# A four-layer graph network on one core: another order for the first quads (projections into the first softmax's wait, W2's sums earlier, the second softmax's sorting in one group)

## The chip, the cores and the metric

The kernel runs on one core of a Trainium2 chip. The metric is the device time of one execution, in microseconds (us). The kernel before takes 3154.85 us (median of three runs, 3150.97 to 3155.34). Every run that was taken in several rounds is on record as fast, that is, not slowed down as a whole. For the times of the five single looks (e2, e3, e4, e7, e9) no state is on record, so I read steps from their traces and conclude nothing from their times.

## The reference, cut to what matters

Four graph layers run on 128 batch elements of 128 nodes with 256 features. Each adds its result to its input and normalises it.

```python
# layer 0: attention over 512 edges (src -> dst), 4 heads
Xq, Xv = x @ W_lin.T, x @ W_val.T
e = sum(leaky_relu(Xq[:, src] + Xq[:, dst]) * a) + log(adj[src, dst] + eps)
attn = softmax of e over the edges with the same src
x = layernorm(x + segment_sum(attn * Xv[:, dst], src) @ W_out.T)
# layer 1: three graph convolutions with adj*adj, W1 (256->512), W2 (512->1024), W3 (1024->256)
# layer 2: three products with W[0..2], mixed by diag / upper / lower part of adj
# layer 3: normalised adj, W1 (256->512), batch norm, relu, W2, batch norm: needs all elements first
```

## The kernel before

Batch elements go in quads of four, 32 quads in all. A loop pass overlaps five quads at different layers; the order of instructions is fixed by hand on every engine. What this study touches is the head: `start()` (quads 0 to 3 up to the softmaxes) and `iteration_0()` (the first, partly filled pass). These are the helpers that the argument needs:

```python
def values_in(k, xg, copy): ...    # TensorE transposes of quad k's input, copies on ScalarE
def values(k, i, copy, ...): ...   # TensorE: projections Xq, Xv of element i; after i == 3 spill Xq to memory
def gather_one(k, t, c, ...): ...  # GpSimd: indirect transfer, chunk c of 128 edges (t=0: src rows, t=1: add dst rows)
def score(k, c, ...): ...          # VectorE, 3.7 us: leaky relu, times a, sum over a head
def sorted_scores(k, perm, ...): ... # TensorE: puts the edges in the order of src
def softmax_parts(k): ...          # generator: scan, scan, subtract (VectorE), Exp (ScalarE), scan, scan
def attention(k): ...              # TensorE transposes, VectorE divides: the attention weights
def scatter(k): ...                # GpSimd: 4 indirect writes, each waiting for the one before; then SyncE loads
                                   # the dense 1 MB attention matrix back
def by_row(k, j, ...): ...         # reorders a quarter of that matrix (ScalarE, or VectorE)
def aggregate(k): ...              # TensorE: attention matrix times values
def second(k, between): ...        # the 1024x512 product W2, 14 parts; between[i]: other work after part i
```

The parts of `start()` and `iteration_0()` in question, with cuts:

```python
            ...
            nc.scalar.activation(weight, weight, AF.Ln)
            score(0, 0)
            ...
            values_in(1, quads[1].xr, nc.scalar.copy)
            ...
            sorted_scores(0, perm, range(NE - 1))
            score(0, NE - 1, ends[:, 3, :])
            sorted_scores(0, perm, (NE - 1,))
            ...  # first softmax
            values_in(2, quads[2].xr, nc.scalar.copy)
            ...
            attention(0)
            values(2, 0, nc.scalar.copy, qt=...)
            scatter(0)
            ...
            score(1, 1, ends[:, 3, :])
            values(3, 1, nc.scalar.copy)
            second_sums()                       # four sums of halves of W2, VectorE
            for j in range(QB):
                by_row(0, j, None if j == 2 else nc.vector.tensor_copy)
            aggregate(0)
            stage_a(0)
            values(3, 2, nc.scalar.copy)
            values(3, 3, nc.scalar.copy)        # its spill goes out on SyncE's queue
            mix1(0, 0)
            ...
            late_loads()                        # layer 2's weights, bias, W3, hidden weights, quad 4, norm vectors
            ...
        def iteration_0():
            late_sums(0)
            between = {i: [] for i in range(14)}
            between[0] = [lambda: attention(1), lambda: scatter(1)]
            for c, i in ((0, 1), (1, 3), (2, 6)):
                between[i].append(lambda c=c: score(2, c))
            between[1].append(lambda: gather_last(2))
            for j, i in enumerate((10, 11, 12, 13)):
                between[i].append(lambda j=j: by_row(1, j))
            second(0, between)
            score(2, NE - 1)
            ...
```

## Time and profile before

| | kernel before |
|---|---|
| median of three runs | 3154.85 us |
| profiled span | 3149.4 us |
| TensorE busy, whole span | 3077.0 us (98%) |
| TensorE idle, 0 to 185 us | 32.9 us |
| TensorE idle, 185 to 3090 us | 27 us |
| first 128x384 product of layer 2 | starts at 175.99 us |

From about 175 us on the program is a steady stream of matmuls. The start of the first 128x384 product of layer 2 is therefore a good mark. Whatever the head gains is the shift of that mark; I call it "the mark" below. The prediction shows and reads the rows of the profile that carry this. One more view matters for what came later. It is SyncE's queue of the kernel before: start, duration, line, transfer.

```profile
61.53 0.34 SPq L427 DMA_DIRECT2D ad<-attd  x1
83.51 0.32 SPq L268 DMA_DIRECT2D qd<-qt  x1
83.88 1.08 SPq L1112 DMA_DIRECT2D l2w<-in_l_w_dram  x2
```

The queue takes its transfers in order. Quad 3's spill (`qd`) waits for projections that are computed near 80 us, so the weight loads behind it start at 83.9 us.

### The profile page before, as it was taken

The page shows a single profiled execution, that of the slowest core. Times are in us where ns is not written, and L with a number is a line of the kernel's source. Part 1 is how long each engine was busy: PE and PEld are TensorE (multiplying, and loading weights), DVE is VectorE, ACT ScalarE, POOL GpSimd, SP SyncE. Part 2 cuts the span into 40 slices and gives each one's busy share as a digit, 9 for nine tenths or more (in the row PEclk, how much of TensorE's full clock was granted, in tenths as well). Part 3 has the DMA queues.
Part 4 walks back from the last instruction along what each step waited for, and adds up shares of the span by engine and source line. Part 5 has one row for each costly group of instructions (what it writes and reads, how often), then busy time and mean ns, then how long its engine had stood idle before and what let it go on. Part 6 is the DMA issues. An engine that isn't in the chain of part 4 may idle for free. (4 is left out here: it accounts for less than half of the span.)

```text
span 3149.4 us, 39744 instructions
## 1 busy us (share of the span) xinstructions
PE 3077.0 (98%) x14752; PEld 2403.3 (76%) x14752; DVE 2306.6 (73%) x4600; ACT 1376.0 (44%) x2548; POOL 651.5 (21%) x535
## 2 busy tenths in 40 slices
PE   7899999999999999999999999999999999989998
PEld 3678888888888888888888888888888887864444
DVE  7777777777777777777777777777777776447888
ACT  3344433444444444334344444444444344326668
POOL 2311222222121111122222211111122220001235
PEclk8999999999999999999999999999999999999999
DMA  5623333333333332333333333332333331005557
GB/s 179 160 68 88 101 108 97 106 108 108 101 86 103 104 91 79 98 108 101 101 108 108 103 94 92 107 91 76 97 108 101 101 108 41 21 31 195 173 195 275
DMA packets 117473, 340.04 MB, mean 108 GB/s; under 512 B 14881, under 2 KB 51617, under 8 KB 108961
## 3 DMA queue, kind: packets, MB, share of 16 engines
q0 software_dynamic: 44544, 147.88, 19.4%
q1 hardware_dynamic: 70976, 188.71, 17.0%
q8 instruction: 117, 1.92, 0.3%
q10 hardware_dynamic: 1760, 0.92, 0.1%
q14 instruction: 76, 0.61, 0.1%
HBM read 252.00 MB, written 85.46 MB: 107 GB/s over the span
## 5 line engine op out<-in xcount | busy, mean ns | idle before, releaser
L575 PE MATMUL ph<-m,w 128*128 128x256 f32 x2048 | 475.0, 380 | 0.0
L655 PE MATMUL p<-w,h 128*128 128x256 f32 x2048 | 463.8, 380 | 0.0
L575 PEld LDWEIGHTS ph<-m,w 128*128 128x128 f32 x2048 | 387.9, 191 | 78.4 <-issue 14.8
L655 PEld LDWEIGHTS p<-w,h 128*128 128x128 f32 x2048 | 389.7, 190 | 67.0 <-issue 8.1
L336 POOL DMA_INDIRECT zs<-qd,src_idx x120 | 117.2, 977 | 1347.8 <-DMA qd<-qt 1216.1
L575 PE MATMUL ph<-m,w_s 128*128 128x256 f32 x1536 | 357.5, 379 | 0.0
L575 PEld LDWEIGHTS ph<-m,w_s 128*128 128x128 f32 x1536 | 291.8, 190 | 52.9 <-issue 14.8
L336 POOL DMA_INDIRECT zs<-qd,dst_idx x120 | 188.1, 1568 | 352.5 <-DMA zs<-qd,src_idx 327.2
L581 ACT COPY u<-ph 128x512 f32<-128x512 f32 x128 | 74.8, 584 | 356.1 <-PE ph L575 356.1
L418 POOL DMA_INDIRECT attd<-at,att_idx x128 | 142.7, 1115 | 347.4 <-DMA attd<-at,att_idx 245.0
L591 ACT ACTIVATE h<-h 128x512 f32<-128x512 f32 x192 | 121.1, 630 | 135.6 <-DVE h L587 135.6
L113 ACT ACTIVATE ln_sd<-ln_mv,eps 128x2 f32<-128x2 f32 x192 | 55.9, 291 | 281.6 <-DVE ln_mv L108 277.8
L370 DVE TENSOR_TENSOR zs<-zs,a_bc 128x1024 f32<-128x1024 f32 x125 | 153.1, 1225 | 4.3
L371 DVE TENSOR_REDUCE scores<-zs 128x16 f32<-128x1024 f32 x125 | 152.5, 1220 | 4.3
L718 ACT COPY x2k<-y 128x384 f32<-128x384 f32 x192 | 92.0, 479 | 138.3 <-PE y L711 113.8
L368 DVE SCALAR_TENSOR_TENSOR zs<-zs 128x1024 f32<-128x1024 f32 x125 | 151.4, 1211 | 0.1
L106 DVE BATCH_NORM_STATS2 ln_st<-xr 128x6 f32<-128x256 f32 x384 | 144.5, 418 | 6.6
L121 DVE TENSOR_SCALAR xr<-xr,ln_mv,ln_rs 128x256 f32<-128x256 f32 x384 | 143.2, 415 | 7.0
L587 DVE TENSOR_TENSOR h<-ph,u 128x512 f32<-128x512 f32 x128 | 87.1, 680 | 73.1 <-PE ph L575 55.0
L437 ACT COPY adc<-ad 128x512 f32<-128x512 f32 x125 | 133.1, 1065 | 4.1 <-DMA ad<-attd 4.1
L679 POOL TENSOR_TENSOR xb<-xr,bias 128x512 f32<-128x512 f32 x64 | 99.3, 1551 | 160.0 <-DVE xr L121 150.7
L532 PE MATMUL pm<-wt_t,h 128*128 128x128 f32 x1024 | 126.7, 277 | 0.0
(342 smaller groups left out, 6071.1 us busy)
## 6 DMA issues: line engine op xcount, KB each, us to landing
ad<-attd SPq DMA_DIRECT2D x32, 1024.0 KB, 4.8
zd<-z SPq DMA_DIRECT2D x31, 1024.0 KB, 7.3
zl<-zd SPq DMA_DIRECT2D x62, 512.0 KB, 3.8
xr<-in_x_dram SPq DMA_DIRECT2D x32, 512.0 KB, 7.5
x3d<-xr SPq DMA_DIRECT2D x32, 512.0 KB, 2.6
x3l<-x3d SPq DMA_DIRECT2D x32, 512.0 KB, 5.1
out_dram<-x3l POOLq DMA_DIRECT2D x31, 512.0 KB
qd<-qt SPq DMA_DIRECT2D x30, 512.0 KB, 2.6
```

The costliest lines, as they stand in the source:

```text
L106: nc.vector.bn_stats(st[:, i, :], r[:, i, :])
L121: nc.vector.tensor_scalar(r[:, i, :], r[:, i, :], mv[:, i, 0:1], rs[:, i:i + 1], op0=ALU.subtract, op1=ALU.mult)
L336: nc.gpsimd.indirect_dma_start(out=s.z[c], out_offset=None, in_=s.qd, in_offset=bass.IndirectOffsetOnAxis(ap=idx[:, c:c + 1], axis=0), com ...
L368: nc.vector.scalar_tensor_tensor(z, z, SLOPE, z, op0=ALU.mult, op1=ALU.max)
L370: nc.vector.tensor_mul(z3, z3, a_bc.unsqueeze(1).to_broadcast([P, QB, D]))
L371: nc.vector.reduce_sum(s.es[:, c, :], z.rearrange("p (r d) -> p r d", d=DH), axis=AX.X)
L418: nc.gpsimd.indirect_dma_start(out=ad, out_offset=bass.IndirectOffsetOnAxis(ap=att_idx[:, c:c + 1], axis=0), in_=s.at[:, c, :], in_offset= ...
L437: (copy or nc.scalar.copy)(s.adc[:, j * H:(j + 1) * H, :], s.ad.rearrange("p (s r) -> p r s", r=R)[:, j * H:(j + 1) * H, :])
L532: nc.tensor.matmul(pm[:, c // 2, c % 2, :], quads[k].h1[i, c], wt_t, start=True, stop=True)
L575: nc.tensor.matmul(bank[g][:, i].rearrange("p b n -> p (b n)"), wa[:, c, f:f + P], s.m2[:, blk_b, c].rearrange("p b n -> p (b n)"), start= ...
L591: nc.scalar.activation(h, h if src_ is None else src_, AF.Relu)
L655: nc.tensor.matmul(p3[:, t * D:(t + 1) * D], s.h2[f // 2][:, f % 2, j + t, :], w3_sb[:, f, :], start=(f == 0), stop=(f == K2 - 1))
```

## The change

The intent is to give TensorE work in its three waits for a softmax and in its wait for the first attention matrix, and to keep its clock up where no work is left. These are the core parts of the diff (small moves and the matching removals are cut):

```diff
+            values_in(1, quads[1].xr, nc.scalar.copy)          # ahead of the logarithm
             nc.scalar.activation(weight, weight, AF.Ln)
...
             score(0, NE - 1, ends[:, 3, :])
+            values_in(2, quads[2].xr, nc.scalar.copy)
             sorted_scores(0, perm, (NE - 1,))
...
+            for i in range(3):
+                values(2, i, nc.scalar.copy, qt=qt2)
             attention(0)
-            values(2, 0, nc.scalar.copy, qt=...)
...
+            for i in range(1, QB):
+                values(3, i, nc.scalar.copy)                   # all of quad 3, ahead of aggregate(0)
...
             second_sums()                                      # both scores of quad 1 now stand ahead of it
+            keep_running(20)                                   # 20 products of ones, result unused
             for j in range(QB):
                 by_row(0, j, None if j == 2 else nc.vector.tensor_copy)
             aggregate(0)
             stage_a(0)
-            values(3, 2, nc.scalar.copy)
-            values(3, 3, nc.scalar.copy)
             mix1(0, 0)
...
-            sorted_scores(1, perm, range(NE - 1))
...
-            sorted_scores(1, perm, (NE - 1,))
+            late_loads()                                       # without W3
...
+            sorted_scores(1, perm)
+            nc.sync.dma_start(w3_sb, w3.rearrange("(c p) f -> p c f", p=P))
...
-            between[0] = [lambda: attention(1), lambda: scatter(1)]
-            for c, i in ((0, 1), (1, 3), (2, 6)):
+            for c, i in ((0, 0), (1, 3), (2, 6)):
                 between[i].append(lambda c=c: score(2, c))
-            between[1].append(lambda: gather_last(2))
+            between[2] += [lambda: attention(1), lambda: scatter(1)]
+            between[3].append(lambda: gather_last(2))
...
-            attention(2)                                       # moved behind w.p3()
-            scatter(2)
```

In the last part the steps of the third softmax are spread between the seven products of `first_seven`. Its Exp stands ahead of the sixth product. One move that is cut above matters later: quad 1's last two gathers (chunks 2 and 3) used to be issued chunk by chunk; now GpSimd issues the first halves of both and then the second halves.

More of the change, by code (lines that the diff above doesn't have):

```diff
@@ L1022, in iteration_0 @@
             mix1(1, 0)
+            next(rest)
             mix1(1, 2)
-            next(rest)
             w = first_seven(1)
             steps = softmax_parts(2)
-            for _ in range(4):
-                next(steps)
+            next(steps)
+            next(rest)
             w.p1()
             next(steps)
+            next(steps)
             run(w.p5, w.p2)
+            next(steps)
+            next(steps)
+            w.p6()
+            next(rest, None)
+            w.p7()
             for _ in steps:
                 pass
-            next(rest)
+            third_mix(0, 2)
+            w.p4()
+            w.p3()
             attention(2)
@@ L1038, in iteration_0 @@
             gather_last(3)
-            w.p6()
-            next(rest, None)
-            w.p7()
-            third_mix(0, 2)
-            w.p4()
-            w.p3()
             quads[0].layer2 = layer2(0, 1)
@@ L1058, in start, with keep_running @@
             nc.scalar.dma_start(a_bc, bass.AP(tensor=a.tensor, offset=a.offset, ap=[[0, P], [1, D]]))
-            warm = ps("warm")[:, :N]
-            for _ in range(10):
-                nc.tensor.matmul(warm, ones, ones, start=True, stop=True)
+            def keep_running(n):
+                warm = ps("warm")[:, :N]
+                for _ in range(n):
+                    nc.tensor.matmul(warm, ones, ones, start=True, stop=True)
+            keep_running(10)
             pos = scratch("pos")
@@ L1114, in late_loads @@
                 nc.sync.dma_start(bias, bass.AP(tensor=l2_bias.tensor, offset=l2_bias.offset, ap=[[0, P], [1, D]]))
-                nc.sync.dma_start(w3_sb, w3.rearrange("(c p) f -> p c f", p=P))
                 nc.sync.dma_start(l3w1, l3_w1_t.rearrange("(c p) f -> p c f", p=P))
@@ L1152, in start @@
             nc.vector.tensor_scalar(es[:, 0, :], es[:, 0, :], ends[:, 3, 0:1], None, op0=ALU.add)
-            values_in(1, quads[1].xr, nc.scalar.copy)
             values(1, 0, nc.scalar.copy)
@@ L1196, in start @@
             sums = wk.tile([P, 6], F32, tag="sums", name="sums", bufs=1)
-            values_in(2, quads[2].xr, nc.scalar.copy)
             pr = ps("adjt_ps")[:, :N]
@@ L1202, in start @@
             nc.vector.tensor_add(an, a_sb, ident)
+            qt2 = l3w1_s.rearrange("p t f -> p (t f)").rearrange("p (b d) -> p b d", d=D)
+            for i in range(3):
+                values(2, i, nc.scalar.copy, qt=qt2)
             attention(0)
-            values(2, 0, nc.scalar.copy, qt=l3w1_s.rearrange("p t f -> p (t f)").rearrange("p (b d) -> p b d", d=D))
             scatter(0)
@@ L1214, in start @@
             nc.vector.reduce_sum(sums[:, 1:2], diag, axis=AX.X)
-            values(2, 1, nc.scalar.copy)
             pr = ps("col_ps")[:, :1]
             nc.tensor.matmul(pr, an, ones[:, 0:1], start=True, stop=True)
+            nc.gpsimd.tensor_copy(small[0][:, 0:1], quads[0].ad[:, 0:1])
+            values(2, 3, nc.scalar.copy, spill_by=nc.gpsimd)
+            for t in range(2):
+                for c in (2, 3):
+                    gather_one(1, t, c, cols_i[:, t, :])
+            values_in(3, quads[3].xg, nc.scalar.copy)
+            score(1, 0, ends[:, 3, :])
             nc.vector.tensor_add(sums[:, 2:3], sums[:, 0:1], pr)
             nc.vector.tensor_sub(sums[:, 3:4], sums[:, 2:3], sums[:, 1:2])
+            values(3, 0, nc.scalar.copy)
             nc.scalar.activation(sums[:, 4:5], sums[:, 3:4], AF.Sqrt)
-            score(1, 0, ends[:, 3, :])
-            values(2, 2, nc.scalar.copy)
-            nc.gpsimd.tensor_copy(small[0][:, 0:1], quads[0].ad[:, 0:1])
-            values(2, 3, nc.scalar.copy, spill_by=nc.gpsimd)
-            for c in (2, 3):
-                for t in range(2):
-                    gather_one(1, t, c, cols_i[:, t, :])
+            score(1, 1, ends[:, 3, :])
             dinv = sums[:, 5:6]
@@ L1231, in start @@
             nc.vector.tensor_scalar(diag, an, dinv, None, op0=ALU.mult)
-            values_in(3, quads[3].xg, nc.scalar.copy)
-            values(3, 0, nc.scalar.copy)
+            for i in range(1, QB):
+                values(3, i, nc.scalar.copy)
             pr = ps("half_ps")[:, :N]
@@ L1236, in start @@
             nc.vector.tensor_scalar(ahat_t, pr, dinv, None, op0=ALU.mult)
-            score(1, 1, ends[:, 3, :])
-            values(3, 1, nc.scalar.copy)
             second_sums()
+            keep_running(20)
             for j in range(QB):
@@ L1243, in start @@
             stage_a(0)
-            values(3, 2, nc.scalar.copy)
-            values(3, 3, nc.scalar.copy)
             mix1(0, 0)
+            first(0, 0)
+            score(1, 2, ends[:, 3, :])
+            first(0, 1)
             mix1(0, 2)
-            score(1, 2, ends[:, 3, :])
-            sorted_scores(1, perm, range(NE - 1))
-            first(0, 0)
+            mixed(0, 0, mix2(0, 0))
+            late_loads()
+            first(0, 2)
             score(1, NE - 1, ends[:, 3, :])
             gather(2)
-            first(0, 1)
-            mixed(0, 0, mix2(0, 0))
-            sorted_scores(1, perm, (NE - 1,))
-            late_loads()
-            first(0, 2)
+            first(0, 3)
             mixed(0, 1, mix2(0, 1))
+            sorted_scores(1, perm)
+            nc.sync.dma_start(w3_sb, w3.rearrange("(c p) f -> p c f", p=P))
+            pm = mix2(0, 2)
             steps = softmax_parts(1)
@@ L1261, in start @@
                 next(steps)
-            first(0, 3)
+            mixed(0, 2, pm)
             next(steps)
-            mixed(0, 2, mix2(0, 2))
             mixed(0, 3, mix2(0, 3))
```

## The prediction

> **What bounds the kernel now.** I read the busy times by stretch first, because the change touches only the head of the program (everything up to the first full loop pass).
>
> ```profile
> 0.00:185.00 185.00, 152.12 (x631) 101.36 (x632) 135.81 (x252) 65.01 (x125) 59.60 (x55) 0.93 0.55 156
> 185.00:3090.00 2905.00, 2878.01 (x13898) 2274.53 (x13897) 2120.92 (x4162) 1258.78 (x2305) 557.55 (x446) 1.00 0.35 102
> 3090.00:3149.40 59.40, 46.92 (x224) 27.42 (x224) 49.89 (x189) 52.24 (x119) 34.39 (x34) 0.94 0.70 253
> ```
>
> After the stretch and its length come the busy times of TensorE, its weight loads, VectorE, ScalarE and GpSimd, then the granted TensorE clock, the DMA share and GB/s. From 185 us to 3090 us TensorE idles 27 us of 2905: that stage is TensorE's, and the change leaves it alone. So the change is worth exactly as much as the start of the full-speed stage moves to the left. In the first 185 us TensorE idles 185 - 152.1 = 32.9 us. The second view is TensorE's waits in these 185 us (total us, times, longest):
>
> ```profile
> PE pat L408 <- DVE pair L400: 14.7, 3, 6.0
> PE py L451 <- DVE adc L437: 7.9, 1, 7.9
> PE pe L360 <- DVE scores L373: 2.7, 2, 1.4
> PE pq L259 <- ACT xt L247: 2.1, 2, 1.8
> PE pm L476 <- DVE xr L121: 1.7, 1, 1.7
> ```
>
> The three waits of the attention transposes for the end of a softmax, and the one wait of the first aggregation for the reordered attention matrix, are 22.6 us of the 32.9. Third, TensorE's timeline shows that a wait also costs afterwards:
>
> ```profile
> 47.75 0.63 PE L408 MATMUL pat<-ident,pair 48*128 48x48 f32 x4 [5.37 <-DVE pair L400]
> 48.31 5.96 PE L259 MATMUL pq<-wqv,xt 128*128 128x512 f32 x8
> ...
> 70.86 3.68 PE L451 MATMUL py<-adc,m 128*64 128x128 f32 x32 [7.90 <-DVE adc L437]
> 74.47 4.85 PE L465 MATMUL po<-wo,yt 128*128 128x256 f32 x16
> 79.16 3.60 PE L259 MATMUL pq<-wqv,xt 128*128 128x512 f32 x8
> ...
> 105.78 0.42 PE L408 MATMUL pat<-ident,pair 48*128 48x48 f32 x4 [3.39 <-DVE pair L400]
> ...
> 161.49 0.63 PE L408 MATMUL pat<-ident,pair 48*128 48x48 f32 x4 [5.97 <-DVE pair L400]
> ...
> 174.59 0.67 PE L697 MATMUL pt<-ident,xr 128*128 128x128 f32 x4 [1.22 <-DVE xr L121]
> ```
>
> Eight projection matmul records take 5.96 us behind the first wait and 3.60 us at 79.16. The fourth view, the clock in short stretches, says why: it is halved there.
>
> ```profile
> 44.00:48.00 4.00, 0.25 (x3) 0.28 (x4) 3.48 (x9) 1.57 (x3) 3.18 (x2) 0.76 0.67 143
> 48.00:52.00 4.00, 4.00 (x9) 1.84 (x9) 2.28 (x9) 0.00 (x0) 1.02 (x1) 0.50 0.95 179
> 72.00:76.00 4.00, 4.00 (x28) 3.40 (x26) 0.00 (x0) 1.17 (x2) 2.59 (x2) 0.50 0.42 55
> ```
>
> From these means the half clock lay over work for about 4.7 us (47.7 to 52.4), 5.9 (70.9 to 76.8), 3.4 (107.5 to 110.9) and 4.0 (161.5 to 165.5): 18 us, half of it lost, 9 us. Idle and cold clock together are 42 us, and that bounds the gain: 42/3155 = 1.3%. A verdict of over 2% is out of reach unless something breaks.
>
> Last, VectorE and ScalarE around the two attention matrices:
>
> ```profile
> 65.46 1.22 DVE L181 TENSOR_TENSOR w_s<-w 128x1024 f32<-128x1024 f32 x1
> ...
> 70.13 1.63 DVE L437 COPY adc<-ad 128x512 f32<-128x512 f32 x3
> ...
> 127.47 1.07 ACT L437 COPY adc<-ad 128x512 f32<-128x512 f32 x1 [1.49 <-DMA ad<-attd]
> ```
>
> ScalarE had its part of the first matrix at 66.29, so the matrix had landed. VectorE reached it only at 70.13, after W2's four sums (4.7 us). The second matrix arrives at 127.4, only just in time.
>
> **What the Trainium skill says.** "TensorE: Matmul & The Clock Gate", Part 1 (the HAM clock gate): after an idle window of about 3.4 us the clock goes to one half, and it needs about 3.4 us of work to come back. The trace agrees: idle from 42.4, half clock from about 46.1, back 4.7 us after work began. The same Part 1 says that ScalarE and VectorE take their instructions strictly in order; the trace agrees (ScalarE's copies of the first transposed inputs stand behind the logarithm at 24.23, and TensorE waits 1.79 us for them). "ScalarE: Activation LUTs", What ACT_TABLE_LOAD costs: about 1283 ns a load; the trace has 1.28 us before each first Exp or Sqrt. It adds a drain of about 1.38 us, of which the trace shows none (load at 156.93, Exp at 158.22). "DMA: Bandwidth & Descriptors", Issuing engines are not separate DMA queues: all share the same engines, so a load let go earlier meets other traffic. DMA shares of 0.95 to 1.05 around 48 to 52 and 100 to 108 show where that can bite.
>
> **The change part by part**, with the durations of the trace, as a schedule in the new program order.
>
> *Copies before the logarithm.* The copies start at 22.9 rather than 24.34, so the 1.79 us wait shrinks to about 0.4. VectorE is solid from 22 to 40 and the softmax still ends at 47.6, so by itself this moves nothing later; it lets quad 1's spill and gathers go about 1.4 us earlier.
>
> *Projections into the first softmax.* Transposes of quad 2 (1.04 us) go into the wait for the last score; three projections (3 x 1.8 = 5.4 us) into 41.5 to 46.9. The 5.37 us wait becomes about 0.9 and the clock stays full. VectorE's attention still ends at 49.2 and the scatter starts at 49.5: the chain scatter, load, reordered matrix is untouched, landing about 66.
>
> *W2's sums ahead.* VectorE does score 0 at 50.4 to 54.1, score 1 at 54.5 to 58.4 (before, it waited 4.07 us for a column sum behind cold projections), then W2's sums at about 59.6 to 64.3. Reordering begins at the landing, 66.2, aggregation at 66.9 rather than 70.86: 4.0 us.
>
> *Twenty warm matmuls.* A 128x128 fp32 product takes 2.01/8 = 0.25 us, so 20 take 4.4 to 5 us. They run at 59.3 to about 64, where TensorE has nothing else, and leave about 3 us idle, which I expect to keep the clock. Aggregation and output product then take 2.0 + 3.6 instead of 3.68 + 4.85: 2.9 us more. Output product ends at 72.5 instead of 79.2; quad 3's two projections (3.6 us) were moved ahead. In return the first mix waits for the layer norm, 1.4 us.
>
> *Second softmax in one group.* The four sorting products (4 x 0.93 us) run together once the last score is there, about 86 to 89.7, with other products before and after. second(0) starts at 91.7 instead of 100.5: 8.8 us ahead. attention(1) stands behind three products (5.2 us) instead of one, so its 3.39 us wait and the cold 1.7 us go too: about 14 us ahead at 98.
>
> *Where it is given back.* After the softmax (pair ready near 97.3) VectorE has two sums (1.4), a whole score of quad 2 (3.7) and a total (0.7) before attention(1): ready at 103.8 against 107.8, only 4 us ahead. From there to the landing took 127.4 - 107.8 = 19.6 us before and 66.3 - 49.2 = 17.1 for the first matrix; I take 17.7, so 121.5. ScalarE reaches its reorder copy near 112 and, being in order, stands on it; the relu copies behind it feed the third weight product. Copies and relus alternate (1.05 + 0.6, twice), so that product's last quarter starts at 124.7, while TensorE is there at 120.4: a new wait of 4 to 5 us. Aggregation of quad 1 ends near 129, against 135.8: 6.8 ahead. VectorE, with quad 2's last score (its gather lands near 125) and 11 us of work behind it, starts the second layer norm at 136.0 against 142.4: 6.4 us ahead.
>
> *The third softmax.* Scans begin after first_seven's sums, 147.2 against 153.7. attention(2) moves behind p6, p7, p4, p3 and two more products (near 6.8 us of work), so most of the 5.97 us wait and the cold 2.0 us go. But Exp with its table load (1.9 us) now stands ahead of a copy that p7 needs: about 2.7 us wait. VectorE runs scans, totals, norm and score to 166.1, where the transposes of the second half start, against 174.6: 8.5 us ahead. From there both programs do the same.
>
> Check by TensorE's own budget. New gaps, us: 1.2 + 0.4 + 0.9 at the start, 0.4 + 1.7 + 0.9 around the first softmax, 0.4, 3.0, 1.4 + 0.7, 0.4 + 1.0, 4.3 + 1.3 at the second matrix, 0.3, 2.7, 0.9, 3.7 = 25.6, plus about 2 of cold clock, plus 4.6 of warm matmuls = 32 against 42. That says 10, the schedule says 8.5; I take 8.5 to 9.
>
> **The rivals.** First, everything goes through: the second matrix comes early enough, or relus are not held by it, and the 14 us won at 98 survive: 3140. For it: idle and cold in the trace are 42 us. Against: the 4 us lead of attention(1), and the chain of four scatters, each waiting for the one before (1.4 to 4 us). Second, the matrix sets it all: only those 4 us arrive, the rest of the lead goes into a longer wait on ScalarE and a cold clock: 3150. For it: ScalarE already waited 1.49 us for that load. Third, let-go loads: quad 3's spill now comes near 60, so the late weight loads, behind it in the queue, start 20 us earlier, beside quad 1's last gathers (3 to 5 us each): the second score comes late, and 1 to 4 us of the gain go: 3149. Against it: the DMA share before was 0.40 in 64 to 68, and the gathers of quad 2 later find a freer engine.
>
> **Range and chances.** The runs of before lie between 3150.97 and 3155.34, so 3154.85 is on their high side; from a middle near 3153.5, minus 8.5, I say 3145. Range 3136 (first rival, plus luck) to 3153 (second or third, plus spread). Faster by over 2% would need 63 us, more than all idle and cold time of the head: 0.005. Slower by over 2% needs a new stall that returns in every pass, and the loop isn't touched: 0.005. Within 2%: 0.99.
>
> **What would show it.** Right: no wait over 1.5 us before the first attention transposes and full clock behind them; aggregation near 67 at full clock; attention(1)'s transposes without a wait; a ScalarE wait of 8 to 10 us for the second matrix and a TensorE gap near 121; the third attention with under 1.5 us of wait; the second-half transposes (174.59 before) near 166. Wrong: a half clock at 67 (then the warm matmuls failed), a wait of the second score for its gather, a second matrix landing after 124 or before 117, or any change of the idle time after 185 us.

## The result

The changed kernel took 3151.35 us (median of 4 runs, 3147.94 to 3152.4), against 3154.8 us before (4 runs). A second comparison with more runs gave 3151.63 us (21 runs, 3146.29 to 3159.08) against 3154.97 us (25 runs, 3149.96 to 3159.94). Ratios here are the mean time of one kernel's fast runs over that of the other's fast runs of the same rounds, so not quite the ratio of the medians. They are 0.999 (95% interval 0.9972 to 1.0007) and 0.9988 (0.9982 to 0.9995). By the tighter one the change saves 0.0012 x 3155 = 3.8 us. That is real, but it is less than half of the 8.5 us that the prediction took off; the time lies in the stated range.

The busy times by stretch after the change, in the columns of the prediction's first view:

```profile
0.00:185.00 185.00, 162.06 (x687) 107.35 (x688) 139.01 (x255) 66.74 (x128) 60.08 (x55) 0.94 0.54 156
185.00:3090.00 2905.00, 2876.14 (x13893) 2272.20 (x13893) 2122.82 (x4167) 1258.87 (x2306) 559.90 (x447) 1.00 0.35 102
```

TensorE's idle time in the first 185 us went from 32.9 to 22.9 us, and 4.6 us of the new busy time are the twenty unused products. Its waits in that stretch:

```profile
PE p L655 <- ACT h L591: 3.7, 1, 3.7
PE y L289 <- ACT adc L506: 3.5, 1, 3.5
PE pt L697 <- DVE xr L121: 2.7, 1, 2.7
PE py L451 <- DVE adc L437: 2.5, 1, 2.5
...
PE pat L408 <- DVE pair L400: 1.4, 2, 1.1
```

The waits for the end of a softmax fell from 14.7 to 1.4 us, and the wait for the first attention matrix from 7.9 to 2.5. In their place stand waits for ScalarE: the third product's for its relu (3.7), and that of a product of `first_seven` for the copy behind Exp (3.5). TensorE's timeline shows where, and two of the rows show something else:

```profile
67.71 1.97 PE L451 MATMUL py<-adc,m 128*64 128x128 f32 x32 [2.53 <-DVE adc L437]
...
77.09 6.73 PE L490 MATMUL ph<-w,mx 128*128 128x512 f32 x8 [1.50 <-ACT mx L479]
...
127.93 2.07 PE L655 MATMUL p<-w,h 128*128 128x256 f32 x4 [3.74 <-ACT h L591]
...
169.25 1.09 PE L697 MATMUL pt<-ident,xr 128*128 128x128 f32 x4 [2.72 <-DVE xr L121]
```

Eight records of the first W1 products take 6.73 us, against 3.70 us for the same eight before. The four transposes at 169.25 take 1.09, against 0.67. The clock of the changed kernel in short stretches says why:

```profile
76.00:80.00 4.00, 2.91 (x4) 1.36 (x5) 1.14 (x6) 0.77 (x2) 1.59 (x1) 0.55 0.60 113
80.00:84.00 4.00, 4.00 (x10) 1.68 (x9) 0.00 (x0) 0.68 (x2) 3.26 (x3) 0.60 0.85 148
```

I read the clock in steps of half a microsecond and summed the busy time at half clock. Before, it lay at 46.0 to 53.0, 66.5 to 77.0, 107.5 to 111.0 and 158.5 to 166.0 us, over 18.5 us of work, so 9.3 us were lost. After, it lies at 49.0 to 52.5, 76.0 to 83.5, 127.5 to 131.0, 158.0 to 162.0 and 168.5 to 172.0, over 18.7 us of work: 9.4 us lost. The waits became shorter, and the loss to the clock did not.

VectorE's timeline shows the two waits for transfers that it did not have before:

```profile
84.28 1.23 DVE L368 SCALAR_TENSOR_TENSOR zs<-zs 128x1024 f32<-128x1024 f32 x1 [6.74 <-DMA zs<-qd,cols_i]
...
107.39 0.22 DVE L412 TENSOR_TENSOR at<-rden,pat 128x64 f32<-128x64 f32 x1
...
128.55 1.23 DVE L368 SCALAR_TENSOR_TENSOR zs<-zs 128x1024 f32<-128x1024 f32 x1 [6.22 <-DMA zs<-qd,dst_idx]
```

Quad 1's third score starts only at 84.28, when its gather has landed. Before, it started at 83.74 without any wait for a transfer, behind VectorE's other work. SyncE's queue of the changed kernel holds the cause that the experiments test:

```profile
61.10 0.34 SPq L427 DMA_DIRECT2D ad<-attd  x1
61.49 0.42 SPq L268 DMA_DIRECT2D qd<-qt  x1
61.97 1.82 SPq L1117 DMA_DIRECT2D l2w<-in_l_w_dram  x2
```

Quad 3's projections were moved ahead, so its spill no longer holds the queue, and the weight loads go out 22 us sooner. They are in flight while the gathers run. GpSimd issues the first half of that gather at 68.52 and sees it landed at 78.23, 9.7 us later; before, the same half took 4.3 us. The rows after the change, and those before it:

```profile
68.52 1.01 POOL L336 DMA_INDIRECT zs<-qd,cols_i  x1 [0.31 <-issue]
69.84 0.94 POOL L336 DMA_INDIRECT z<-qd,cols_i  x1 [0.30 <-issue]
78.23 1.59 POOL L336 DMA_INDIRECT zs<-qd,cols_i  x1 [7.46 <-DMA zs<-qd,cols_i]
```
```profile
67.79 1.04 POOL L336 DMA_INDIRECT zs<-qd,cols_i  x1 [0.31 <-issue]
72.07 1.60 POOL L336 DMA_INDIRECT zs<-qd,cols_i  x1 [3.24 <-DMA zs<-qd,cols_i]
```

Side by side, with the prediction's own numbers:

| event (us) | before | predicted | after |
|---|---|---|---|
| first aggregation starts | 70.86 | 66.9 | 67.71 |
| second sorting ends | 94.3 | 89.7 | 93.9 |
| second(0) starts | 100.5 | 91.7 | 95.73 |
| weights of attention 1 ready | 107.8 | 103.8 | 107.6 |
| second attention matrix used | 127.47 | 121.5 | 124.87 |
| last quarter of the third product | about 133 | 124.7 | 127.93 |
| layer norm of quad 1 starts | 142.44 | 136.0 | 139.61 |
| second-half transposes | 174.59 | 166.1 | 169.25 |
| the mark | 175.99 | not given | 171.84 |

Up to the first aggregation the schedule holds within a microsecond. At the second sorting the kernel is 4.2 us later than predicted, and it stays 3 to 4 us late. At the second-half transposes the lead over before is 5.3 us, at the mark 4.15 (the half clock from 168.5 took the rest). Followed at the first product of every loop pass, it is 4.1 us at 210 us and 3.1 us at 2772 us; most of the difference goes in one pass near 940 us. The last 375 us differ from trace to trace of one kernel: from the pass at 2772 to the end they took 374.2 us in the trace of before, 378.6 in this one and 376.2 in the second trace of the changed kernel (e1 below). That is why the profiled run of the changed kernel is not shorter at all (3150.7 against 3149.4).

### The profile page after: what moved, and what is told of

The parts are those of the page before. It is cut to its first block, busy times and chain, and to the rows that moved or that the text cites. A ratio compares the mean times of both kernels' runs of the same rounds, so it can differ in the third digit from the quotient of the medians.

```text
span 3150.7 us, 39824 instructions
## 1 busy us (share of the span) xinstructions
PE 3083.1 (98%) x14792; PEld 2406.8 (76%) x14792; DVE 2310.7 (73%) x4600; ACT 1376.2 (44%) x2548; POOL 653.6 (21%) x535
```

## The experiments

Twelve runs. With one exception each is the changed kernel with one edit, or with several. The mark in a single trace moves by a microsecond or two with the half clock. A run "in rounds" was executed many times, together with the kernel before; the others were executed once. So I read the step that an edit is about first, and the time only where there were several rounds. All twelve gave correct results.

**1. The changed kernel again (e1), five rounds.** No edit.

> The changed kernel once more, unaltered, to learn how far one trace and one time can be trusted. My theory: the head's lead over the kernel before, read at the first 128x384 product of layer 2 (175.99 us before, 171.84 after), repeats within 1 us, so a lead of 3.5 to 5 us, while the total time scatters by 2 us from one execution to the next; ratio 0.9975 to 1.000. Rival (the first trace was a chance state of the clock): the marker moves by over 2 us, because the half clock falls elsewhere.

Measured: 3151.63 us, ratio 0.9988 (0.9982 to 0.9995), the 21 runs quoted above. The mark came at 173.49, 1.65 us later than in the first trace and only 2.5 us ahead of before, so the hope of 1 us was too tight. So was that of 2 us for the time: the 21 runs lie between 3146.29 and 3159.08. In this trace the half clock lay elsewhere: not at 49 and 76, but at 67.5 to 71.5 and 95.0 to 98.5, and at 170.0 to 177.0. These are TensorE's rows:

```profile
68.14 3.43 PE L451 MATMUL py<-adc,m 128*64 128x128 f32 x32 [4.29 <-DVE adc L437]
...
78.98 3.70 PE L490 MATMUL ph<-w,mx 128*128 128x512 f32 x8 [1.51 <-ACT mx L479]
```

The projections ran at full clock here, so the twenty unused products were done sooner. The gap behind them grew from 2.53 to 4.29 us, and the first aggregation ran at half clock after all. The rival holds in part: where the half clock falls differs between two traces of the same kernel, and the sum lost is much the same (9.6 us).

**2 to 4. What makes the second sorting late: the loads, the clock, or both?**

```diff
 # e2: late loads behind W3's load, which waits for the sorting
-            late_loads()
...
             nc.sync.dma_start(w3_sb, w3.rearrange("(c p) f -> p c f", p=P))
+            late_loads()
 # e3: unused products into the two small gaps
             stage_a(0)
+            keep_running(4)
             mix1(0, 0)
+            keep_running(5)
             first(0, 0)
 # e4: both
```

> Changed kernel, but the late weight loads (layer 2's weights, bias, hidden weights, quad 4's input) are put behind the load of W3, which waits for the second softmax's sorting, near 94 us. Theory 'two limits side by side' (the second sorting is held by quad 1's late gather, landing 84.3, and at once by TensorE running the first products at half clock until 82): VectorE's 6.74 us wait for the gather falls under 2 us (score of chunk 2 starts at 77 to 79), but TensorE still reaches the sorting at about 90, the first scan starts at 93 to 94 as before, and the marker stays within 1 us of 171.84. Rival 'the loads alone': the first scan starts at 89 to 91 and the marker comes at 167 to 169. Rival 'not the loads' (the gather is late for another reason): VectorE's wait stays over 5 us.

> Changed kernel with four warm 128x128 products ahead of the first mix of quad 0 and five between it and the first W1 product, into the two idle spots of 1.1 and 1.5 us. Theory 'two limits': the first W1 products take 1.8 us each rather than 3.4 and TensorE is at the sorting at about 86, but waits there for the score (gather still late): first scan at 93 to 94, marker within 1 us of 171.84. Rival 'the clock alone': first scan at 90 to 91, marker 168 to 169.5. If the nine products do not hold the clock, 4 matmul records of the first W1 product still take over 3 us and the run says nothing of the rivals.

> Both edits of the two runs ahead of this one. Theory 'two limits': only now the first scan of the second softmax moves, to 89 to 91, the second attention matrix lands near 121, and the marker comes at 167.5 to 169.5, 3 to 4 us ahead of the changed kernel. Each single-cause rival says that this run equals the one with its own edit alone, within 1 us.

Measured in e2: VectorE's wait fell from 6.74 to 2.09 us (score at 79.89). But then it waited 2.71 us for TensorE, whose first W1 products were again at half clock, and the first scan came at 92.26, the mark at 172.24 (3147.67 us, one run). In e3 these products took 3.70 us and the score still waited for its gather until 85.05: scan at 94.73, mark at 172.32 (3149.04 us, one run). In e4 VectorE's rows read:

```profile
80.50 1.23 DVE L368 SCALAR_TENSOR_TENSOR zs<-zs 128x1024 f32<-128x1024 f32 x1 [2.68 <-DMA zs<-qd,cols_i]
...
90.74 1.21 DVE L389 TENSOR_TENSOR_SCAN m<-reset_f,pe 16x512 f32<-16x512 bf16 x1 [1.09 <-PE pe L360]
```

The first scan comes at 90.74, 3.2 us sooner than in the changed kernel, and the mark at 169.66 (3147.81 us, one run), just outside the expected range. The second matrix was used at 124.06, not near the expected 121: from the first to the fourth scatter it took 9.76 us rather than 8.64, and from there to the use 9.63 rather than 8.35. So little of the 3.2 us reached the mark in this trace, which also lost 2 us less to half clock. So two limits lay side by side. Either edit alone leaves the other limit standing, and both together move this step, the sorting, by about what the prediction missed. e2's scan came somewhat sooner than its theory said, because only one window of half clock fell there, not two. The later traces fill the same table, since the half clock came or stayed away by chance:

| first scan of the second softmax (us) | W1 products at half clock | at full clock |
|---|---|---|
| loads from 62 us on | 93.95 (changed), 93.71 (e5), 94.12 (e6) | 95.00 (e1), 94.73 (e3), 94.42 (e7), 95.78 (e10) |
| loads elsewhere | 92.26 (e2) | 90.74 (e4), 90.41 (e8), 89.91 (e9), 89.87 (e11) |

With the loads in the way, full clock over the W1 products moved the scan no sooner: the gather decided (in e7 and e10 half clock also fell on the sorting itself). With the loads elsewhere the clock is worth about 2 us; that rests on one trace against four.

The gather shows the loads' cost more directly. From its issue at 67.5 to 68.9 to its landing, that first half took 8.9 to 10.6 us in the seven traces with the loads in the way, and 5.3 to 5.8 us in the five without (e2, e4, e8, e9, e11). The rest of the way to the 4.3 us of before may be the new order of the gathers; no run takes that order back.

**5. Are the twenty products worth something? (e5), three rounds.**

```diff
-            keep_running(20)
```

> Changed kernel without the twenty warm products ahead of the first aggregation. Theory (quad 1's late gather is the gate behind that stage, so warmth there buys nothing): the first aggregation runs at half clock (py over 3.4 us, as before the change), the layer norm is 2 to 3 us later, but the score of chunk 2 still starts at 83.5 to 85.5, when its gather lands, and the marker (first 128x384 product) stays at 171 to 174; ratio to the kernel before 0.998 to 0.9995, that of the changed kernel (0.9988). Rival (the fillers carry the gain): marker 174 to 177, ratio 0.9992 to 1.0005.

Measured: 3150.32 us (20 runs), ratio 0.999 (0.9983 to 0.9996). The first aggregation took 3.68 us at half clock, the layer norm began 1.4 us later (73.08 against 71.64; 2 to 3 were expected), and the scan came at 93.71, the mark at 172.51. The score started at 82.48, a little before the expected range. So the fillers buy no time that shows. The reason that the theory gave fits only in part: in this trace the scan waited 2.08 us for TensorE, so the gather was not the last gate.

**6. Attention 1 ahead of the score (e6), three rounds.** Only VectorE's order changes.

```diff
-            for c, i in ((0, 0), (1, 3), (2, 6)):
-                between[i].append(lambda c=c: score(2, c))
             between[2] += [lambda: attention(1), lambda: scatter(1)]
+            for c, i in ((0, 2), (1, 3), (2, 6)):
+                between[i].append(lambda c=c: score(2, c))
```

> Changed kernel with attention 1 and its scatter ahead of quad 2's first score on VectorE (TensorE's order is the same). Theory (the second attention matrix is the gate of the second sorting's gain): the attention weights are ready 3.2 to 3.7 us sooner after the softmax ends (gap from the last scan's start to the weights 3.5 to 4.5 rather than 7.4 us), the load lands that much sooner, TensorE's wait for the relu in the third product falls from 3.7 to under 1.5 us, the marker comes at 167.5 to 170.5; ratio 0.997 to 0.9985. Rival (the displaced score hurts as much): totals of second(0) hold TensorE for 2 us or more, or quad 2's last score is later than 128.5, and the marker stays at 171 to 174.

Measured: 3146.62 us (18 runs), ratio 0.9977 (0.997 to 0.9984). The second sorting was as late as before this edit (scan at 94.12), but the weights were ready at 104.1 rather than 107.6, and the matrix was used at 121.99. This is TensorE's row for the third product:

```profile
125.09 1.13 PE L655 MATMUL p<-w,h 128*128 128x256 f32 x4 [0.74 <-ACT h L591]
```

The wait fell from 3.74 to 0.74 us, and no half clock followed. The mark came at 168.68, 3.2 us ahead of the changed kernel. No loss from the score that gave way shows. This theory stands: behind the sorting, the way to the second attention matrix sets the pace.

**7. Exp behind the copy (e7), one look.**

```diff
             next(steps)
-            next(steps)
             w.p6()
+            next(steps)
```

> Changed kernel with the third softmax's Exp behind the sixth product's copy on ScalarE, not ahead of it. Theory: TensorE's 3.47 us wait for that copy falls to 1 to 2 us (the copy then waits for the relu at 154.6 alone), Exp is 0.5 us later, and since VectorE's scans wait for the Exp and for the seventh product's total, the second-half transposes come 1.5 to 2 us sooner measured from the layer norm of quad 1 (29.6 us from its first addition at 139.61 to 169.25 in the changed kernel; 27.6 to 28.3 expected). Rival: the wait only moves to the attention transposes, and that span stays within 0.5 us of 29.6.

Measured: the wait for the copy fell from 3.47 to 1.54 us, but a wait of 1.27 us for another ScalarE copy, now behind Exp, came up at 157.53. From the layer norm (139.65) to the second-half transposes (168.38) it took 28.7 us rather than 29.6. The gain is 0.9 us, half of what was expected; the wait has partly moved on. The mark was 169.82 (3146.03 us, one run).

**8. All of these together (e8), five rounds.** The edits of e4, e6 and e7, and 28 rather than 20 products.

> Late loads behind W3, the nine fillers, 28 rather than 20 products ahead of the first aggregation, attention 1 ahead of the score, Exp behind the copy. If the theories of the single runs hold and add up: first scan of the second softmax at 89 to 91.5, second matrix landed by 119 to 122, marker at 163.5 to 168, that is 8 to 12 us ahead of the kernel before; ratio 0.9962 to 0.9978. If each only moves the wait on: marker 168 to 171, ratio 0.998 to 0.999.

Measured: 3148.22 us (13 runs), ratio 0.9984 (0.9976 to 0.9992), what was expected if each edit only moves the wait on, and no better than e6 alone, whose interval overlaps. The mark came at 172.11, later than either expectation. The scan came at 90.41 and the weights were ready at 100.4, both as hoped. But the matrix was used only at 123.58, 23 us later. GpSimd's rows show the first scatters:

```profile
100.69 1.76 POOL L418 DMA_INDIRECT attd<-at,att_idx  x1 [10.01 <-DVE at L412]
107.73 1.00 POOL L418 DMA_INDIRECT attd<-at,att_idx  x1 [5.28 <-DMA attd<-at,att_idx]
```

GpSimd waited 5.28 us for the first scatter rather than 1.92. The late loads, started at 90.8, kept the transfer engines full until about 106. They had been moved out of one indirect transfer's way and into another's. But that is not the whole delay. From the first to the fourth scatter it took 3.1 us longer than in e6 (12.28 against 9.17), and from there to the use of the matrix another 2.2 us longer (10.61 against 8.42), when the loads were long through (columns as in the prediction's first view):

```profile
116.00:120.00 4.00, 4.00 (x20) 3.54 (x19) 0.69 (x1) 0.00 (x0) 0.00 (x0) 1.00 0.92 367
120.00:124.00 4.00, 0.64 (x3) 0.21 (x2) 0.00 (x0) 0.42 (x1) 0.34 (x1) 1.00 0.06 24
```

From 120.5 to 123 the DMA share stood at 0.06, as much as one busy engine of sixteen gives. Why the end of the transfer was so slow is open.

TensorE's wait in the third product grew to 6.00 us. My expectation had not asked what the loads would meet next.

**9. The loads where the engines are idle (e9), one look.** Between 28 and 36 us almost nothing is moved in the changed kernel. All late loads but quad 4's input go to about that place (they ran at about 24 to 30):

```diff
             nc.sync.dma_start(w2_sb, w2.rearrange("(c p) f -> p c f", p=P))
+            # layer 2's weights, bias, hidden weights, norm vectors
...
-            late_loads()
...
             scatter(2)
+            quads[4].xg = load_x(4, "xg", 1, xpool)
```

> Changed kernel with the late weight loads (layer 2's weights, bias, hidden weights, norm vectors) issued behind W2's load instead, so that they run near 24 to 32 us where the transfer engines were almost idle, and quad 4's input behind the third scatter. In the run with the loads behind W3, and more so in the combined run, the second attention matrix took longer from its weights to the landing (18.1 and 23.4 us instead of 17.3 to 17.5). Theory (the loads cost whatever indirect transfers they meet): now both are free of them: the score of chunk 2 starts at 77 to 80.5, and weights to landing takes 16.5 to 17.6 us. Rival (scatter time does not depend on the loads): it stays at 18 or more. Marker 169 to 172, TensorE's half clock deciding within that.

Measured: the score started at 79.42, the scan came at 89.91 (the clock happened to be full), the weights were ready at 103.6, and the matrix was used at 120.85, 17.3 us later. The mark was 168.80, 3.0 us ahead of the changed kernel (3148.14 us, one run). Both indirect transfers are free of the loads. With this one edit, and a clock that happened to be full over the W1 products, the rest of the prediction's schedule was met within a microsecond: weights 103.6 (103.8 predicted), matrix 120.85 (121.5), last quarter of the third product 123.92 (124.7), layer norm of quad 1 at 135.75 (136.0), second-half transposes 166.33 (166.1). It is one trace, and this edit alone was not timed in rounds.

```profile
123.92 2.07 PE L655 MATMUL p<-w,h 128*128 128x256 f32 x4 [3.77 <-ACT h L591]
...
166.33 0.97 PE L697 MATMUL pt<-ident,xr 128*128 128x128 f32 x4 [2.71 <-DVE xr L121]
```

**10. The combination without moving loads (e10), three rounds.**

> The combined kernel without its move of the late loads (fillers, attention 1 first, Exp behind the copy; loads where the change has them). Theory: weights to landing back to 17 to 18.5 us, landing near 121 to 122, TensorE's wait in the third product under 1.5 us, marker 165.5 to 168.5, ratio 0.997 to 0.9978. Rival (the fillers or the Exp order spoiled the combination): marker 171 to 174 as in the combined run.

Measured: 3147.93 us (17 runs), ratio 0.9981 (0.9974 to 0.9988); the mark came at 170.53. The third product's wait was 0.75 us as expected. But the gather landed at 85.24, the scan came at 95.78, and half clock lay over 93 to 100 us, so the matrix was used at 124.75. The expected gain over e6 did not come: in this program fillers and Exp order are worth nothing that shows.

**11. The combination with early loads (e11), five rounds.**

> All edits with the early loads in place of the moved ones. Theory: weights of attention 1 ready at 99.5 to 101, landed near 117 to 118.5, before TensorE needs it (wait in the third product under 1 us), quad 2's last gather landed by 121, marker at 161.5 to 165, 11 to 14 us ahead of before; ratio 0.9955 to 0.997. If another wait takes over (the head's VectorE chain), marker 165 to 168 and ratio 0.997 to 0.9978.

Measured: 3144.67 us (6 runs, 3138.62 to 3147.27), ratio 0.9969 (0.9956 to 0.9981), some 10 us under the kernel before. Its TensorE rows:

```profile
122.52 2.08 PE L655 MATMUL p<-w,h 128*128 128x256 f32 x4 [2.41 <-ACT h L591]
...
163.10 0.81 PE L711 MATMUL y<-l2w,x2t 128*128 128x384 f32 x2
```

The mark is at 163.10, 12.9 us ahead of before; the traced execution was the fastest of the six (3138.62). Half clock was left in one stretch only (122.0 to 126.0, 1.7 us lost). The matrix was used at 119.45, a microsecond later than expected, so the wait was 2.41 us, not under 1: from the fourth scatter to the use it took 10.12 us, against 8.38 in e9. Why is not shown; the last gather of quad 2 shares the engines with this load, but it does so in e9 too. It is the fastest version of the study. With six runs its interval is wide, and it still overlaps that of e6.

**12. The early loads in the kernel before (e12), five rounds.** The same edit of the loads, with nothing of the change; W3's load stays where it was.

> The kernel BEFORE with nothing altered but the early weight loads (and quad 4's input behind the third scatter). Before, VectorE never waited for quad 1's last gathers and the loads ran at 84 to 108 us. Theory (the collision is one that the change made, by letting the loads go at 62 us; before, they met nothing that set the pace): the marker stays within 1.5 us of 175.99 and the ratio is 0.999 to 1.0005. Rival (early loads are a gain by themselves, and the change has little to do with it): marker 170 to 174, ratio 0.9975 to 0.9988, about the 3.5 us that the same edit gave on the changed kernel's trace.

Measured: 3155.16 us (14 runs), ratio 1.0005 (0.9995 to 1.0014); the mark came at 174.04. The time says that early loads are worth nothing there. The mark moved 1.95 us, half a microsecond more than I had allowed. Most of that lead was there before the loads start in the kernel before (83.9): the first aggregation was 1.0 us sooner and the first layer norm 1.5 us. The rival's 170 to 174 is just missed too, and its ratio clearly. So the collision with the gather is one that the change made. The loads of the kernel before do meet its scatters, which took 11.11 us from the first to the fourth there and 8.91 here, but nothing on TensorE waited for that.

## Why the prediction was right, and where its size was off

**Right: the bound, the class and the sign.** Idle time and cold clock of the head were 42 us, so over 2% was out of reach, and the loop was untouched. The gain is clear of noise with 21 runs. That the time fell inside the stated range proves little: its upper end, 3153, was set for the second and third rivals and lies only 2 us under the median of before. Of the 6 us by which 3145 was missed, about 1.5 come from the start, a middle of 3153.5 where 25 runs give 3154.97. Two of the prediction's own signs of being wrong came true, the second score's wait for its gather (6.74 us) and a second matrix after 124 (124.87), and in e1 a third, the half clock at 67.

**Right: the first part.** First softmax: a wait of 1.09 us was measured against 0.9. W2's sums: aggregation at 67.71 against 66.9. The clock held there in the first trace, though not in the second. One detail was wrong at once: half clock at 49.0 to 52.5, where "the clock stays full" was said.

**Wrong in size: the second softmax's sorting.** The step that failed is "the four sorting products run together once the last score is there, about 86 to 89.7". They ended at 93.9. The third rival had named the cause ("let-go loads": the spill near 60, the loads 20 us earlier, beside quad 1's last gathers) and given it 1 to 4 us. It came at the upper end, and the main line had counted none of it. The prediction's argument against it, a DMA share of 0.40 at 64 to 68 us before, was the share without the loads. After, the share there was 0.96. With the loads elsewhere and full clock over the W1 products the scan came at 89.9 to 90.7 (e4, e8, e9, e11): the prediction's figure.

**Wrong in size: the clock.** "Plus about 2 of cold clock" measured 9.4. The other terms of that sum were good: idle 25.6 predicted, 22.9 measured; fillers 4.6 and 4.6. So the sum was 36.9 rather than 32, against 42.2 before, and the 10 us of the check became 5.3, the lead at the second-half transposes. The prediction judged a gap by its own length (about 3 us ahead of the first aggregation, "which I expect to keep the clock"); at the first W1 products two gaps of 1.1 and 1.5 us close together were followed by half clock.

**Right: what comes behind.** From the weights of attention 1 to the use of the matrix: 17.3 us measured, 17.7 predicted. Here luck helped: the prediction took this from the first matrix without asking why it had been 19.6 before. The scatters had met the late loads, and the early start that delayed the gather cleared their way (18.1 us in e12, where only the loads moved). New wait of the third product: 3.74 against 4 to 5. Wait for the copy behind Exp: 3.47 against 2.7. Wait of the second-half transposes: 2.72 against 3.7. These steps carried the 4 us of lateness through, almost unchanged, to the mark.

**Of the rivals**, the first (everything goes through) failed for the reason that the prediction gave, the way to the second matrix; e6 shows what that was worth, 3.2 us. The second (only that way matters) was right about the gate, but its 3150 assumed a lead of 4 us at the weights where there was none.

Open: what exactly a filler is worth at each place, since single traces differ by where half clock falls; what cost 0.9 us in one loop pass near 940 us; what the new order of the gathers costs; and why the second matrix took some 2 us longer at its end in e8 and e11.

## What to carry to other kernels

When work is moved ahead on one engine, look at what stood behind it in a transfer queue that works in order: moving the projections let 2 MB of loads go 22 us sooner, into the way of the gathers that set the pace. Put such loads into a stretch where the trace shows idle transfer engines, and ask again what they meet there; moving them a second time without asking left the combination no better than one of its parts. Where two limits end at nearly the same time, removing one shows nothing: test both together before dropping either.

## What the Trainium skill lacked or had wrong

- "TensorE: Matmul & The Clock Gate", Part 1 (the HAM clock gate), ties the half clock to an idle window of about 3.4 us; it also says that frequent short idle times between groups of matmuls can bring it, but gives no size for them. Here gaps of 1.1 and 1.5 us with a 1 us product between them were followed by half clock in 4 of the 7 traces in which no products were put into these gaps (changed kernel, e2, e5, e6), and in none of the 5 with them (e3, e4, e8, e10, e11). So a stretch that was only partly idle was enough. The page's window itself agrees: read in half-microsecond steps, stretches of half clock lasted 3.5 to 4, 7 to 7.5 or 10.5 to 11 us, near one, two or three windows. So does its remark that the window runs freely: the same kernel traced twice had them in different places. For the single gap ahead of the first aggregation, up to 3.2 us kept the clock and 4.2 us or more lost it. That is no threshold: in the third product a gap of 2.41 us was followed by half clock (e11) and one of 3.12 was not (e7).
- "DMA: Bandwidth & Descriptors", Issuing engines are not separate DMA queues, says that transfers interleave, but no page gives a size for what plain loads cost an indirect transfer. Here half a gather took 8.9 to 10.6 us to land beside 2 MB of loads (seven traces; 9.7 in the changed kernel) and 5.3 to 5.8 us without them (five traces). GpSimd's wait for a scatter was 5.28 us beside them (e8) rather than 1.92.
- "ScalarE: Activation LUTs", What ACT_TABLE_LOAD costs, adds about 1.38 us of drain to a load of 1.28 us. No trace here shows it: in the changed kernel the load starts at 154.58 and Exp at 155.87.
